# A four-layer network on one core: the scans of layer 0 written out as slots, with the other layers' work passed through them

## The chip, the core and the metric

The kernel runs on one core of a Trainium2 chip. A core has five engines that this text names as the profile does: PE (TensorE, matrix products, with its weight loads as PEld), DVE (VectorE), ACT (ScalarE), POOL (GpSimd) and SP (SyncE, which here only issues transfers). Each works through its own list of instructions in the order of the program and waits on semaphores for the others. The metric is the device time of one execution in microseconds; several executions are timed and their median is given.

## What is computed

The input x is 4 images of 384 channels and 48 x 48 pixels in float32. Four layers follow, each `x = x + layer(group_norm(x))`:

```python
# layer 0: a state-space scan over the 2304 pixels of an image
xz = xs @ in_proj_w.T;  xin, z = split(xz)          # 768 inner channels each
xin = silu(causal_conv4(xin) + conv_b)
dt, B, C = split(xin @ x_proj_w.T)                   # B, C: 16 states
dt = softplus(dt @ dt_proj_w.T + dt_proj_b)
h[t] = exp(dt[t] * A) * h[t-1] + dt[t] * B[t] * xin[t]   # per channel and state
y[t] = sum over states of h[t] * C[t]
out  = layer_norm(((y + xin * D) * silu(z)) @ out_proj_w.T)
# layer 1: 1x1 product, a filter on 8x8 patches in the frequency domain,
#          3x3 depthwise convolution, gelu(x1) * x2, 1x1 product
# layer 2: 11x11 depthwise convolution with kernels made of 4 points
# layer 3: 4 experts, relu(x @ w1 + b1) @ w2 + b2, top 2 by a gate per pixel, weighted
```

Layer 3 as the reference has it weighs expert e by whether *any* pixel has it first (or second), so that with all experts in use the weights of the two choices add to one for each expert and the layer is the plain sum of the four experts; the kernels compute the sum, look at a flag, and take the weighted way only if the flag asks for it.

## The kernel before

*The scans.* `scans` (line 411) runs over 20 pieces `i = (b, t)`: 4 images, each cut into five fifths of 460 or 464 pixels. The 768 inner channels are six groups of 128, taken as three pairs `p`; 16 states. So there are 20 x 96 = 1920 units `unit(i, m, s)` (line 618), each one scan of 128 channels over one fifth for one state. A unit is: ACT makes the decay `da = exp(dt * a)` in PSUM (line 629); POOL makes the drive `bu = u * B` (633); DVE scans (637), into `da` in place, or, for one unit in three, into `g`; the product with C is DVE's (643) for the two and POOL's (655) for the one, whose four transposes are added to `y` two units late (`late`); ACT copies the last column to `carry` (645, 654); PE adds `g` to `y` in PSUM by four transposes against the identity (`turned`, 587, recorded at line 591). `bc` holds B and C of a state, broadcast to all partitions by a transfer (625).

*The work around them.* Each fifth also has projections of the next (`project`, `project_z`), `gates` (silu), `expand` and `steps` (dt, u), `gate`, `out_proj`, `layer_norm` and `residual` of the one before. `plan(q, piece)` puts each piece behind unit q of the fifth, whole, from its first matmul to its last DVE operation. `scans` is a generator: it yields after each unit, and the main loop at line 1218 puts in pieces of the other layers, by weights and a steady rate, from unit 24 of an image on: `later(b-1)` (line 799, layers 1 and 2 and the gate's scores of layer 3 of the image before) and, ahead of it in the same list, `experts(b-2)` (line 1107, layer 3 of the image before that; the weights of all four experts are held, and `output` adds the four experts of a block of 144 pixels in one PSUM bank).

*The order on an engine* is not that of the text: a scheduling layer orders instructions by its own estimates and priorities, with `after` (line 395) and `high_priority` to bind a few, and `table_back` to return ACT to the table set of exp and ln.

*After the last scan* (line 1241 on) come `later(3)` mixed with `experts(2)`, then the routing, then `experts(3)`.

*Buffers:* PSUM has eight banks: three `da`, two `y`, two for all products (`mm`), one for long sums (`A`). In SBUF `g` has six buffers, `bu` three, `bc` four.

## Time and profile before

| | us |
|---|---|
| median of 3 runs | 5739.81 (5737.92 to 5743.05) |
| profiled execution, its own time | 5734.58 |
| its span, first to last instruction | 5732.5 |
| PE busy, PEld busy | 4867.7, 3805.7 |
| DVE busy | 4006.7 |
| ACT busy, POOL busy | 3044.1, 3104.5 |
| mean granted clock of PE | 0.884 of full |

A page of the profile gives each engine's busy time, then the span in 40 slices with a digit for the busy tenths of each engine, the clock that PE was granted and what the transfers did, then the chain of waits that ended last, and the groups of instructions: line, engine, operation, out<-in, how often, busy time, mean length in ns, and the idle time before them with what ended it. Matmuls are pipelined and their ends are modelled, so that a busy PE is not a PE at its peak. The records of a float32 matmul come in two for each instruction of the program; transposes come singly.

```profile
L1156 PE MATMUL ph<-xe,w 128*128 128x144 f32 x4608 | 620.8, 288 | 7.3 <-DVE dt L582 4.1
L1174 PE MATMUL pout<-hr,w 128*128 128x144 f32 x4608 | 617.8, 287 | 2.0 <-DVE xe L1185 1.9
...
L1164 ACT ACTIVATE hr<-ph,nb 128x144 f32<-128x144 f32 x768 | 235.4, 376 | 498.4 <-PE ph L1156 498.2
L895 DVE SCALAR_TENSOR_TENSOR dw<-pad,w_dw,dw 128x384 f32<-128x384 f32 x576 | 345.0, 614 | 20.2 <-ACT pad L883 16.1
```

These are the experts' two products, their relu, and the taps of the depthwise convolution of layer 1.

### The profile page before, as it was taken

The numbers are of one execution on the slowest core, as the hardware profiler recorded it, in microseconds if no ns is written. First come the engines' busy times: TensorE is split into PE (matmuls) and PEld (weight loads), VectorE is DVE, ScalarE is ACT, GpSimd is POOL, SyncE is SP. The second block draws the span as 40 slices with busy tenths as digits, with TensorE's granted clock in tenths as the row PEclk, the third lists the DMA queues.
The fourth block names the chain that finished last, engine by engine and source line by source line (L and its number), as shares of the span: only waits on it lengthen the run. The fifth ranks groups of instructions, "written<-read, shape, count | busy, mean of one in ns | idle before, by whom it ended". The sixth has DMA issues, their size and how long they took to land. (4 is left out here: it accounts for less than half of the span.)

```text
span 5732.5 us, 78378 instructions
## 1 busy us (share of the span) xinstructions
PE 4867.7 (85%) x27796; PEld 3805.7 (66%) x27796; DVE 4006.7 (70%) x5653; ACT 3044.1 (53%) x6658; POOL 3104.5 (54%) x2795
## 2 busy tenths in 40 slices
PE   6677777877788979999667988999867888999999
PEld 3555555544466657888444876989644576789999
DVE  5989898898897887667786777657787776351110
ACT  3555555556476665455554675545544675335321
POOL 3988888765576775556552666646553576000000
PEclk9778877978799989999768898999977799999999
DMA  4444444333344453333332335333332233311100
GB/s 134 137 143 144 141 127 142 124 114 116 98 150 138 128 178 124 109 109 121 101 112 84 114 117 173 107 95 116 113 100 70 95 128 126 113 56 39 47 23 26
DMA packets 396048, 634.78 MB, mean 111 GB/s; under 512 B 32374, under 2 KB 386790, under 8 KB 392191
## 3 DMA queue, kind: packets, MB, share of 16 engines
q1 hardware_dynamic: 382148, 618.58, 33.8%
q10 hardware_dynamic: 13498, 11.11, 0.6%
q8 instruction: 220, 3.60, 0.3%
q14 instruction: 182, 1.48, 0.1%
HBM read 571.80 MB, written 57.80 MB: 110 GB/s over the span
## 5 line engine op out<-in xcount | busy, mean ns | idle before, releaser
L633 POOL TENSOR_TENSOR bu<-u,bc 128x460 f32<-128x460 f32 (+1 forms) x1920 | 2209.2, 1168 | 1065.7 <-DVE g L637 488.3
L591 PE MATMUL y<-ident,g 128*115 128x128 f32 (+1 forms) x7680 | 1262.0, 313 | 433.1 <-DVE g L643 426.8
L591 PEld LDWEIGHTS y<-ident,g 128*115 128x115 f32 (+1 forms) x7680 | 1088.0, 199 | 673.3 <-DVE g L643 537.6
L629 ACT ACTIVATE da<-dt,a_neg 128x460 f32<-128x460 f32 (+1 forms) x1920 | 1221.9, 646 | 229.2 <-DVE g L643 141.7
L637 DVE TENSOR_TENSOR_SCAN da<-da,carry,bu 128x460 f32<-128x460 f32 (+1 forms) x1008 | 1158.0, 1172 | 152.1 <-ACT da L629 79.0
L655 POOL TENSOR_TENSOR g<-g,bc 128x460 f32<-128x460 f32 (+1 forms) x660 | 767.8, 1163 | 306.3 <-DVE g L637 122.9
L643 DVE TENSOR_TENSOR g<-da,bc 128x460 f32<-128x460 f32 (+1 forms) x1260 | 766.3, 628 | 90.2 <-PE y L591 76.8
L637 DVE TENSOR_TENSOR_SCAN g<-da,carry,bu 128x460 f32<-128x460 f32 (+1 forms) x528 | 617.5, 1169 | 129.6 <-PE y L591 92.6
L1156 PE MATMUL ph<-xe,w 128*128 128x144 f32 x4608 | 620.8, 288 | 7.3 <-DVE dt L582 4.1
L1174 PE MATMUL pout<-hr,w 128*128 128x144 f32 x4608 | 617.8, 287 | 2.0 <-DVE xe L1185 1.9
L1156 PEld LDWEIGHTS ph<-xe,w 128*128 128x128 f32 x4608 | 590.2, 192 | 24.1 <-issue 7.8
L1174 PEld LDWEIGHTS pout<-hr,w 128*128 128x128 f32 x4608 | 585.4, 190 | 17.7 <-issue 9.3
L1015 PE MATMUL pc<-band,row 128*128 128x162 f32 (+14 forms) x3456 | 494.5, 297 | 34.4 <-ACT row L1004 30.1
L1015 PEld LDWEIGHTS pc<-band,row 128*128 128x128 f32 x3456 | 472.0, 205 | 60.4 <-ACT row L1004 39.2
L645 ACT COPY carry<-da 128x1 f32<-128x1 f32 x1008 | 154.5, 157 | 671.9 <-DVE g L643 668.4
L1164 ACT ACTIVATE hr<-ph,nb 128x144 f32<-128x144 f32 x768 | 235.4, 376 | 498.4 <-PE ph L1156 498.2
L895 DVE SCALAR_TENSOR_TENSOR dw<-pad,w_dw,dw 128x384 f32<-128x384 f32 x576 | 345.0, 614 | 20.2 <-ACT pad L883 16.1
L515 PE MATMUL pinz<-xch,w_inz 128*128 128x460 f32 (+1 forms) x720 | 319.4, 581 | 38.6 <-DVE dt L582 14.3
L687 PE MATMUL po<-w_out,zs 128*115 128x384 f32 (+1 forms) x960 | 338.5, 502 | 12.8 <-DVE xc L504 7.2
L487 PE MATMUL pin<-xch,w_inx 128*128 128x463 f32 (+2 forms) x720 | 329.8, 595 | 11.5 <-DVE xc L504 6.0
L637 DVE TENSOR_TENSOR_SCAN da<-da,nil,bu 128x460 f32<-128x460 f32 x252 | 289.0, 1172 | 48.6 <-ACT carry L645 15.9
L1185 DVE SCALAR_TENSOR_TENSOR xe<-pout,b_sum,xe 128x144 f32<-128x144 f32 x192 | 58.9, 360 | 343.9 <-PE pout L1174 343.9
(173 smaller groups left out, 5331.9 us busy)
## 6 DMA issues: line engine op xcount, KB each, us to landing
bc<-bcd SPq DMA_DIRECT2D x768, 460.0 KB, 3.7
bc<-bcd SPq DMA_DIRECT2D x192, 464.0 KB, 3.6
xs<-x1d SPq DMA_DIRECT2D x24, 576.0 KB, 3.9
x2d<-xs SPq DMA_DIRECT2D x24, 576.0 KB, 2.9
x<-x2d SPq DMA_DIRECT2D x12, 1152.0 KB, 8.3
x3d<-x SPq DMA_DIRECT2D x12, 1152.0 KB, 6.1
xg<-x3d SPq DMA_DIRECT2D x24, 576.0 KB, 4.0
xe<-x3d SPq DMA_DIRECT2D x64, 216.0 KB, 2.6
```

The lines of the kernel that those rows point to most:

```text
L487: nc.tensor.matmul(ps[:, lo : halo + n], lhsT=w_inx[:, k, bass.ts(j, P)], rhs=c["x"][:, k, lo : halo + n], start=k == 0, stop=k == CT - 1,)
L591: nc.tensor.matmul(y[:w, bass.ts(k, P)], lhsT=src[:, bass.ts(k, w)], rhs=ident, is_transpose=True, start=start and k == 0, stop=stop, skip ...
L629: nc.scalar.activation(da[:, :n], c["dt", p][:, m % 2, :n], AF.Exp, scale=a_neg[:, m, s : s + 1])
L633: nc.gpsimd.tensor_mul(bu[:, :n], c["u", p][:, m % 2, :n], bc[:, 0, :n])
L637: nc.vector.tensor_tensor_scan(here[:, :n], da[:, :n], bu[:, :n], last if t else nil[:, 0:1], ALU.mult, ALU.add,)
L643: nc.vector.tensor_mul(g[:, :n], here[:, :n], bc[:, 1, :n])
L655: nc.gpsimd.tensor_mul(g[:, :n], here[:, :n], bc[:, 1, :n])
L687: nc.tensor.matmul(ps[:w, :C], lhsT=c["zs"][:, m, bass.ts(k, w)], rhs=w_out0[:, m, :], start=m == 0, stop=m == MT - 1,)
L895: nc.vector.scalar_tensor_tensor(v, src, w_dw[:, ct, k : k + 1], v, ALU.mult, ALU.add)
L1015: nc.tensor.matmul(d["acc2"][:, : BANDS[k] * W].rearrange("p (h w) -> p h w", w=W)[:, lo - edges[k] : hi - edges[k], xlo:xhi], lhsT=d["row ...
L1156: nc.tensor.matmul(ps[:, bass.ts(m, EB)], lhsT=d["w1"][:, e, k, bass.ts(m, P)], rhs=d["x", s][:, k, :], start=k == 0, stop=k == CT - 1,)
L1174: nc.tensor.matmul(d["o"][:, bass.ts(m, EB)], lhsT=d["w2"][:, e, k, bass.ts(m, P)], rhs=d["h", s, e][:, k, :], start=e == 0 and m == 0 and ...
```

## The change

Every piece of work is rewritten as a generator of *steps*. A step names its engine, and for PE a weight (about its us), a PSUM buffer that must be free, and a condition. `Ring` counts buffers as read or not; `Task` is one piece with the pieces that it needs; a `Lane` holds a queue of tasks and lets up to `width` of them move one step a slot, PE steps with weight against a credit that grows by `rate` a slot. The 1920 units become slots `u` in one loop under `manual_schedule`: the order of the text is the order on each engine.

In slot u: ACT steps of all lanes; copies of finished `y`; the scan of u with its product; the decay of u+2; the drive of u+3; POOL's product of u-1; the adds of u-4 (POOL's product) or u-2; then the PE, DVE, POOL and transfer steps of all lanes; `bc` seven units ahead. PSUM is now two `da`, two `y`, three `mm`, one `acc`; `g` has five buffers, `bc` five, `xch` two, and several buffers of layers 1 and 2 one instead of two.

Three lanes: `aux` for layer 0's own work (`plan` gives each task a first slot and what it needs), `one` for `later(b-1)`, `two` for `experts(b-1)`, which begins when `later(b-1)` has ended. In `experts` one expert runs over the whole image before the next: its weights alone are held, expert 0 writes x plus its part and all biases to `y3d` in HBM, each further one reads and adds to it, the last writes the output. The last image's layer 3 (`all_experts`) is as before. In layer 1 the taps of the third channel group come before those of the second, so that both gelus stand together, with one table change; the residual input is fetched again as `xr`. Weights for `fold` are issued on SP instead of ACT.

```diff
+class Lane:
...
+    def step(self, act, slot=0):
+        if not act:
+            self.credit = min(self.credit + self.rate, 4.0)
+        for task in self.active:
+            if task.ended:
+                continue
+            kind, weight, ring, when = task.next
+            if (kind == "act") != act or (weight and self.credit <= 0):
+                continue
+            if (ring and not ring[0].free(ring[1])) or (when and not when()):
+                continue
+            self.credit -= weight
+            task.move()
...
             def project(i, j):
...
+                yield ("pe", 0, (ring, 1))
...
-                ps = bank(f"pin{b}_{t}_{j}")
+                ps, r = ring.take(f"pin{b}_{t}_{j}")
...
+                yield ("act",)
...
+                yield ("dve",)
                 for k in range(halo):
...
+                ring.done(r)
...
+            def where(u):
+                i, q = divmod(u, LEN)
+                p, q = divmod(q, PAIR)
+                return i, p, 2 * p + q % 2, q // 2, q % 3 == 0
...
+            def scan(u):
...
+                here = g if slow else da
                 nc.vector.tensor_tensor_scan(
                     here[:, :n], da[:, :n], bu[:, :n], last if t else nil[:, 0:1],
                     ALU.mult, ALU.add,
                 )
...
+                if not slow:
+                    nc.vector.tensor_mul(g[:, :n], da[:, :n], live["bc", u // 2][:, 1, :n])
+                if t < NC - 1:
+                    nc.scalar.copy(last, here[:, n - 1 : n])
...
+                for u in range(N + 5):
...
+                    for lane in (aux, *lanes):
+                        lane.step(True, u)
+                    for h, e in ((1, u - 3), (0, u - 4)):
+                        if 0 < e < N and e % PAIR == PAIR - 1:
+                            collect(e, h)
+                    if u < N:
+                        scan(u)
+                    if u + 2 < N:
+                        decay(u + 2)
+                    if u + 3 < N:
+                        ready(u + 3)
+                        drive(u + 3)
+                    if 0 < u <= N:
+                        product(u - 1)
+                    add(u - 4, True)
+                    add(u - 2, False)
+                    for lane in (aux, *lanes):
+                        lane.step(False, u)
+                    if u % 2 and u + 7 < 2 * (N // 2):
+                        spread((u + 7) // 2)
...
+                def taps(ct):
+                    yield ("dve", 0, (accr, 1))
...
+                    room = 3 if slow_slot() else 2
+                    for k in range(9):
+                        if not room:
+                            yield ("dve",)
+                            room = 3 if slow_slot() else 2
+                        room -= 1
...
+            def block(s, e):
...
+                yield ("pe", 2.2, (ring, 1), lambda: hrs.free())
+                ps, r = ring.take(f"ph{b}_{s}_{e}")
+                h, hk = hrs.take(f"hr{b}_{s}_{e}")
+                product(ps, d["w1"], x)
...
+                yield ("act",)
...
+                yield ("pe", 2.2, (ring, 1))
+                ps, r = ring.take(f"pout{b}_{s}_{e}")
+                product(ps, d["w2"], h)
+                hrs.done(hk)
+                yield ("dve",)
+                if e:
+                    x, yk = d["y", s, e]
+                    y = x.rearrange("p c t -> p (c t)")
+                    nc.vector.tensor_add(y, ps[:, : CT * EB], y)
...
+        rings = of_experts("xe", 2), of_experts("ye", 2), of_experts("hr", 1)
...
+        ring, accr = psum("mm", 3), psum("acc", 1)
+        one, two = Lane(6), Lane(3)
+        one.rate, two.rate = 0.75, 0.62
...
+            holder[0], ring.n, accr.n = mm, 6, 2
+
+            one.queue += later(NB - 1, ring, accr)
+            one.rate, two.rate = 4.0, 0.45
```

After the scans the manual order ends; `later(3)` and `experts(2)` go through the lanes again, and the scheduling layer orders the engines there as before.

## The prediction

> **What bounds the kernel now.** I read the page first, then busy time by stage, then the costliest groups, then single instructions of VectorE in order of time.
>
> ```profile
> PE 4867.7 (85%) x27796; PEld 3805.7 (66%) x27796; DVE 4006.7 (70%) x5653; ACT 3044.1 (53%) x6658; POOL 3104.5 (54%) x2795
> ...
> PE   6677777877788979999667988999867888999999
> ...
> DVE  5989898898897887667786777657787776351110
> ...
> PEclk9778877978799989999768898999977799999999
> ...
> PE 11%; issue 4%; DVE 1%; DMA 0%; ACT 0%; SPq 0%; POOL 0%; DVEq 0%; ACTq 0%; POOLq 0%
> ```
>
> The reader sees two limits that take turns: where the PE row shows 9 the DVE row falls to 6 or 5, and where DVE shows 8 or 9, PE shows 6 to 8 at a lowered clock. The chain of waits is no help: it reaches back only to about 4789 us. So I cut the run at the first scan of each image (the starts of scans 0, 480, 960 and 1440 in the trace are 95.9, 1007.6, 2127.7 and 3487.2 us; the last scan ends at 4828.3) and asked for the busy time in these stretches.
>
> ```profile
> 95.00:1008.00 913.00, 680.55 (x2923) 476.39 (x2922) 826.67 (x1030) 525.59 (x1124) 768.27 (x686) 0.79 0.43 138
> 1008.00:2128.00 1120.00, 918.66 (x4559) 649.03 (x4557) 968.40 (x1346) 688.54 (x1457) 775.75 (x695) 0.87 0.40 129
> 2128.00:3487.00 1359.00, 1175.90 (x6904) 930.83 (x6902) 1000.32 (x1392) 756.44 (x1658) 778.53 (x698) 0.89 0.36 114
> 3487.00:4828.00 1341.00, 1160.08 (x6830) 912.25 (x6829) 978.01 (x1346) 742.75 (x1636) 773.37 (x693) 0.89 0.35 112
> 4828.00:5733.00 905.00, 879.38 (x6427) 804.39 (x6425) 202.63 (x472) 305.89 (x751) 4.82 (x15) 0.97 0.16 51
> ```
>
> The second and third fifth of image 2, by the same view:
>
> ```profile
> 2369.00:2640.00 271.00, 268.14 (x1921) 237.60 (x1920) 179.18 (x237) 141.52 (x355) 154.98 (x137) 1.00 0.35 109
> 2640.00:2945.00 305.00, 228.36 (x1035) 155.35 (x1034) 237.97 (x348) 156.12 (x328) 155.39 (x144) 0.81 0.34 108
> ```
>
> The columns are PE, PE's weight loads, DVE, ACT, POOL, clock, DMA share and rate. Image 0 is near VectorE's limit (91%). In images 1 to 3 VectorE is busy only 77% of 3820 us, although in total it has as much to do as any engine: experts(b-2) come in one burst (271 us with PE at 99%), then layers 1 and 2 come in another (305 us with DVE at 78%). The last stretch, 905 us, is PE at 97%.
>
> Of the groups, the drive's product on GpSimd and the readout's product on VectorE:
>
> ```profile
> L633 POOL TENSOR_TENSOR bu<-u,bc 128x460 f32<-128x460 f32 (+1 forms) x1920 | 2209.2, 1168 | 1065.7 <-DVE g L637 488.3
> ...
> L643 DVE TENSOR_TENSOR g<-da,bc 128x460 f32<-128x460 f32 (+1 forms) x1260 | 766.3, 628 | 90.2 <-PE y L591 76.8
> ```
>
> VectorE in order of time (start, length, both in us), inside image 0:
>
> ```profile
> 508.91 1.17 DVE L643 TENSOR_TENSOR g<-da,bc 128x460 f32<-128x460 f32 x2
> 509.98 1.17 DVE L637 TENSOR_TENSOR_SCAN g<-da,carry,bu 128x460 f32<-128x460 f32 x1
> 511.48 1.18 DVE L637 TENSOR_TENSOR_SCAN da<-da,carry,bu 128x460 f32<-128x460 f32 x1 [0.33 <-POOL bu L633]
> 512.75 0.64 DVE L643 TENSOR_TENSOR g<-da,bc 128x460 f32<-128x460 f32 x1
> ```
>
> And a line of the chain of waits that prices PE:
>
> ```profile
> 4986.08 2.21 PE pout L1174 x18
> ```
>
> A scan starts at 509.98, 0.10 us before the two products of 1.17 us from 508.91 end; but the product at 512.75 starts 0.09 us after the scan from 511.48 (1.18 us) ends, because it reads that scan's result. Over the whole trace, neighbours on DVE that don't need each other overlap by 85 to 93 ns (medians), a product right behind its own scan starts 91 ns after it (160 cases), and a tap or other fused multiply-add behind the one it continues starts 35 ns after it. PE at full clock: 18 matmuls of 144 columns in 2.21 us, 123 ns each. In the same way, start to start at full clock: a transpose of g 109 ns, 384 columns 323, 460 columns 387.
>
> **What the Trainium skill says.** "Perfetto Trace Analysis", Optimization Strategy: where the most contended engine changes over time, interleave the regimes; the stage lines above show two such regimes. "VectorE: DVE Perf Modes", The DRAIN you can't avoid: the next operation waits until the pipe is empty, and one that isn't held starts earlier; the trace agrees in both halves (91 ns behind, 90 ns ahead). "TensorE: Matmul & The Clock Gate", Part 1: the clock is half or full, and activity releases it; the trace shows 1.00 in the burst and 0.79 in image 0. "PSUM — Partial Sum Buffer", Engine vs sequencer instructions: the queues of ScalarE, VectorE and GpSimdE are strictly first in, first out; the DVE records start in the program's order throughout. So a step laid out too early holds up everything behind it on its engine.
>
> **The change part by part.**
>
> *Unchanged:* the 95.9 us before the first scan. Neither kernel has expert work of image 2 before the last scan in its PE order; after it stand later(3), experts(2), experts(3): 834 us of matmuls at full clock before, 828 after (same gaps, counts from the two orders). Before took 905 us for it. After adds in this tail 48 additions of `ye` (lines of 128x432, an estimate of 0.6 us from 128x384 and 128x460 rows, beside PE), one hidden buffer instead of three (about 0.1 us in 64 blocks, 7 us), and weights that are fetched per expert into the only buffer: the chain shows 10.3 us for such a fetch (`w<-in_L_w2T`). Mostly hidden behind later(3). I take 912 us, from 895 to 950.
>
> *DVE gets dearer.* Before, the scheduler put other work between most scans and their products (160 of 1260 stand directly behind). After, all 1260 do: 1100 x (91 + 93) ns = +202 us. More chained taps and similar pairs: about +55 us. Experts one by one: 96 additions of `ye` in the scan stage, less 90 ns overlap, 96 x 0.51 = +49 us, and small biases, +14. DVE's work from first to last scan, priced so: 3715 us before, 4036 after. By image: 816, 961, 980, 958 before; 875, 1037, 1075, 1049 after.
>
> *ACT and SP.* Table loads 141 to 91, 50 x 1.28 = 64 us less, off the path except that one gelu block per strip now stands in front of the decays. Silu still holds ACT for 2 x 2.5 + 2 x 1.28 = 7.6 us once a fifth. SP gets 470 more DMAs (`y3d`, `ye`, `xe` again, `xr`), about 100 MB on 635; the DMA engines are 34% busy, `bc` is fetched seven slots ahead (median landing 3.7 us against 2.3 us a slot): nothing.
>
> *PE work is spread.* By image at full clock, before and after: 494/502, 746/745, 1028/1039, 1011/1008. The totals don't move; their place inside an image does. Fifths of image 2: before PE 220, 265, 163, 201, 180 against DVE 169, 172, 235, 229, 175; after 191, 208, 196, 231, 213 against 208, 254, 230, 192, 191.
>
> *The sum.* Each engine's order is a list of slots: 1920 scans, with what stands between two of them. I priced every slot on each engine by the rows above, took groups of slots, and added the largest engine's total of each group: the group's size stands for how far engines can run apart (three to six buffers). With PE at 0.95 of full clock (0.87 to 0.89 in images 1 to 3, but 1.00 wherever PE is the limit), before gives 4599 us in groups of six and 4912 in groups of four; it took 4732. The mean of both, 4755, is within 0.5%. After gives 4485 and 4654, mean 4570: by image 911, 1127, 1286, 1247 against 912, 1120, 1359, 1341 measured before. The new layout has two `da` buffers for three, five `g` for six, and no scheduler to fill holes; I add 20 us and take 4590. Sum on the profile: 96 + 4590 + 912 = 5598 us against 5732.5. The profiled run was 5734.6 us (2 above its span), the median of the runs 5 more: 5605 us.
>
> **Rivals.**
>
> *In-order stalls (slower).* Place: ACT's lane steps stand in front of the decay for two slots on, and wait for PE steps of the slot before; every third product (line 839 of the new code) needs PE to be less than two slots behind. A slot with a project (6 x 0.387) and a block (18 x 0.123) is 5 us of PE with its transposes, double at half clock; ACT then stops, and DVE two slots later. Then engines run apart by two slots at most: groups of two give 5053 us, total 6061; half way to groups of four, 4850, total 5865. It decides from 0.07 us a slot on (4725 - 4590 over 1920). For it: DVE and PE are both loaded 2.1 us a slot in images 2 and 3. Against it: each step is laid one slot behind its producer, and `ring` lets three banks be in flight instead of two. I price it at 5880.
>
> *Balance pays in full (faster still).* PE stays at full clock since it is never idle long: groups of six at full clock, 4411, total 5426. Against it: image 0 has no work to spread and its DVE work grew by 59 us.
>
> *Gain eaten exactly.* DVE's +320 us equals what the spreading frees: 5728 to 5752 of the median, a narrow case. That the change doesn't do what it says I exclude: the orders show expert blocks of image 0 from slot 975 to 1427, beside later(1) from 1017 on.
>
> **How the numbers follow.** Likeliest, faster by 1 to 4%: 46%, 5605, own range 5480 to 5725. Faster still: 12%, 5430. Stalls: 37%, 5880, up to 6061. No change: 5%. Under 0.2% (12 us) this measurement can't tell from no change, as the three runs lie within 5 us. So faster 0.58, same 0.05, slower 0.37. The range leaves out some 15 in 100: it runs from 5420 (groups of six, full clock) to 6010 (most of the stalls' case).
>
> **What would show it.** Right: DVE busy over 84% in images 1 to 3 (77% now), no stretch with PE at 99% before the last scan, products directly behind scans with 91 ns between, image 0 between 900 and 940 us, the last stretch near 912. Wrong: ACT's decay or DVE's scan waiting for PE or ACT in each slot, clock under 0.85 in images 2 and 3, image 0 over 960 us, or a tail over 950 with PE waiting for weights.

## The result, and the profile after

The changed kernel takes 5829.09 us (median of 4, 5826.41 to 5839.95) against 5741.43 us (4 runs, 5737.92 to 5744.53) for the kernel before: ratio 1.0156, 95% interval 1.0139 to 1.0174. It is slower by 1.6%, where 5605 us, faster by 2.4%, was forecast. The profiled execution took 5827.99 us, its span is 5825.9.

The page of the changed kernel, the same rows as before:

```profile
PE 4837.9 (83%) x27796; PEld 3792.9 (65%) x27796; DVE 4239.6 (73%) x5806; ACT 3007.6 (52%) x6632; POOL 3119.5 (54%) x2795
...
PE   6677667777768898887889998888889998889999
...
DVE  5889888989988778788987778788977874631200
...
PEclk8788778788879898998989999888989999999999
...
PE 14%; DVE 1%; ACT 1%; DMA 1%; issue 0%; POOL 0%; SPq 0%; ACTq 0%; DVEq 0%; POOLq 0%
```

The swing between two limits inside images 1 to 3 is gone, as intended: DVE shows 7 to 9 from the second slice to the last scan, and PE 7 to 9 from the thirteenth slice on. The stretch after the last scan, called the tail below (the last seven digits), shows PE at 8 in three slices, where before it had 9 but for its start. DVE's total grew by 233 us. By stages, cut at the first scan of each image (87.7, 1061.3, 2248.8, 3570.5 us; last scan ends at 4852.3), with the columns of the prediction:

```profile
87.70:1061.30 973.60, 690.63 (x2960) 481.31 (x2960) 854.29 (x1036) 533.75 (x1122) 770.29 (x684) 0.79 0.41 129
1061.30:2248.80 1187.50, 923.80 (x4554) 657.57 (x4554) 1019.89 (x1348) 685.27 (x1450) 780.99 (x699) 0.85 0.39 126
2248.80:3570.50 1321.70, 1159.58 (x6948) 919.97 (x6948) 1064.45 (x1450) 746.00 (x1656) 782.23 (x698) 0.93 0.48 147
3570.50:4852.30 1281.80, 1127.22 (x6800) 897.15 (x6800) 1040.04 (x1395) 729.28 (x1631) 777.30 (x693) 0.92 0.47 145
4852.30:5826.00 973.70, 889.64 (x6384) 806.76 (x6384) 233.00 (x520) 290.23 (x741) 4.38 (x14) 0.96 0.28 82
```

| | before | forecast | after | after - before |
|---|---|---|---|---|
| before the first scan | 95.9 | 95.9 | 87.7 | -8 |
| image 0 | 911.7 | 911 | 973.6 | +62 |
| image 1 | 1120.1 | 1127 | 1187.5 | +67 |
| image 2 | 1359.5 | 1286 | 1321.7 | -38 |
| image 3 | 1341.1 | 1247 | 1281.8 | -59 |
| after the last scan | 904.2 | 912 | 973.6 | +69 |
| allowance for fewer buffers | | 20 | | |

So spreading the experts did pay in images 2 and 3, 97 us instead of the forecast 168, at a higher clock (0.93 and 0.92, from 0.89). Images without experts, 0 and 1, and the tail lost 198 us.

The records of VectorE give an account of the four images. Call its *own time* what it is busy, with the short gaps of up to 0.15 us between two of its instructions, and *waits* all longer gaps. From the first scan to the last its own time grew by 304 us (3798 to 4103; by image 53, 79, 88, 85), and its waits fell by 272 us (934 to 662; by image +9, -11, -126, -145). The difference is the 32 us that this stretch got longer. So the spreading freed VectorE of waits, and its dearer work is a little larger than what that freed. This is an account, and doesn't by itself show how much of the 304 us has to reach the time; the experiments ask that.

The product behind its scan, in order of time (start, length):

```profile
504.09 0.64 DVE L839 TENSOR_TENSOR g<-da,bc 128x460 f32<-128x460 f32 x1
504.64 1.17 DVE L834 TENSOR_TENSOR_SCAN g<-da,carry,bu 128x460 f32<-128x460 f32 x1
505.73 1.16 DVE L834 TENSOR_TENSOR_SCAN da<-da,carry,bu 128x460 f32<-128x460 f32 x1
506.98 0.64 DVE L839 TENSOR_TENSOR g<-da,bc 128x460 f32<-128x460 f32 x1
```

The scan at 505.73 ends at 506.89, its product starts 0.09 us later; the scans at 504.64 and 505.73 start 0.09 and 0.08 us before what precedes them ends. Over the trace all 1260 products start 91 ns (median) behind the operation before them; in the kernel before, where 523 had a scan of some unit directly ahead, the median of these began 86 ns before that scan's end.

What VectorE waits for over the whole run (who waits <- for whom: us, times, longest), the four that the experiments turn on:

```profile
DVE ye L1554 <- PE pout L1526: 291.2, 92, 21.4
...
DVE xc L654 <- ACT xc L648: 149.2, 93, 5.6
DVE da L834 <- ACT da L810: 103.4, 73, 6.3
DVE lst L901 <- ACT on L897: 79.3, 45, 5.6
```

The wait for `xc` was 45.8 us before. Both `xc` and `lst` are steps whose ACT half and DVE half stand in the same slot: the ACT steps of a slot come first, and the DVE step that needs one can follow at the end of the same slot. Before's waits of scans and products for PE to free `g` (115.8 and 76.8 us) are almost gone (2.4 and 0.4).

### The profile page after: what moved, and what is told of

It is laid out like the page before. It is cut to its first block, busy times and chain, and to the rows that moved or that the text cites. A ratio compares the mean times of both kernels' runs of the same rounds, so it can differ in the third digit from the quotient of the medians.

```text
span 5825.9 us, 79675 instructions
## 1 busy us (share of the span) xinstructions
PE 4837.9 (83%) x27796; PEld 3792.9 (65%) x27796; DVE 4239.6 (73%) x5806; ACT 3007.6 (52%) x6632; POOL 3119.5 (54%) x2795
## 5 line engine op out<-in xcount | busy, mean ns | idle before, releaser
L821 POOL TENSOR_TENSOR bu<-u,bc 128x460 f32<-128x460 f32 (+1 forms) x1920 | 2225.2, 1168 | 1567.1 <-DVE da L834 986.3
L810 ACT ACTIVATE da<-dt,a_neg 128x460 f32<-128x460 f32 (+1 forms) x1920 | 1243.9, 648 | 328.4 <-DVE g L839 231.0
L834 DVE TENSOR_TENSOR_SCAN da<-da,carry,bu 128x460 f32<-128x460 f32 (+1 forms) x1008 | 1181.0, 1172 | 145.0 <-ACT da L810 95.7
L839 DVE TENSOR_TENSOR g<-da,bc 128x460 f32<-128x460 f32 (+1 forms) x1260 | 803.2, 637 | 93.7 <-PE y L763 0.4
L834 DVE TENSOR_TENSOR_SCAN g<-da,carry,bu 128x460 f32<-128x460 f32 (+1 forms) x528 | 616.0, 1167 | 20.3 <-ACT da L810 17.3
L1526 PE MATMUL pout<-hr,w 128*128 128x144 f32 x3456 | 504.4, 302 | 33.4 <-ACT hr L1542 19.4
L1526 PEld LDWEIGHTS pout<-hr,w 128*128 128x128 f32 x3456 | 475.3, 203 | 61.2 <-ACT hr L1542 28.0
L1526 PE MATMUL ph<-xe,w 128*128 128x144 f32 x3456 | 495.0, 300 | 20.5 <-DMA xe<-x3d 7.4
L1526 PEld LDWEIGHTS ph<-xe,w 128*128 128x128 f32 x3456 | 469.6, 201 | 43.5 <-issue 16.5
L635 PE MATMUL pin<-xch,w_inx 128*128 128x463 f32 (+2 forms) x720 | 368.6, 656 | 34.8 <-DVE xc L654 22.9
L654 DVE SCALAR_TENSOR_TENSOR xc<-pin,conv_w,xc 128x460 f32<-128x460 f32 (+1 forms) x360 | 250.6, 696 | 157.8 <-ACT xc L648 149.2
L1542 ACT ACTIVATE hr<-ph,nb 128x144 f32<-128x144 f32 x576 | 176.1, 376 | 344.1 <-PE ph L1526 344.1
```

What stands on the lines that cost most here:

```text
L635: nc.tensor.matmul(ps[:, lo : halo + n], lhsT=w_inx[:, k, bass.ts(j, P)], rhs=c["x"][:, k, lo : halo + n], start=k == 0, stop=k == CT - 1,)
L810: nc.scalar.activation(da[:, :n], c["dt", p][:, m % 2, :n], AF.Exp, scale=a_neg[:, m, s : s + 1])
L821: nc.gpsimd.tensor_mul(bu[:, :n], c["u", p][:, m % 2, :n], live["bc", u // 2][:, 0, :n])
L834: nc.vector.tensor_tensor_scan(here[:, :n], da[:, :n], bu[:, :n], last if t else nil[:, 0:1], ALU.mult, ALU.add,)
L839: nc.vector.tensor_mul(g[:, :n], da[:, :n], live["bc", u // 2][:, 1, :n])
L1526: nc.tensor.matmul(ps[:, bass.ts(m, EB)], lhsT=w[:, k, bass.ts(m, P)], rhs=of[:, k, :], start=k == 0, stop=k == CT - 1,)
```

## Experiments

The theories: **A**, VectorE's dearer work (the product behind its own scan above all) decides. **B**, VectorE stands in line behind steps whose ScalarE or PE half is late. **C**, the tail's loss comes from weights in one buffer and a single `hr`; later **C2**, from PE standing in line there. **D**, engines can run apart by two to three slots only, so that each engine's work reaches the time by its share of the chain of waits. For D, I followed the chain back from the last scan of each image in the trace of the changed kernel: VectorE has some 471 of 973 us of it in image 0, 514 of 1187, 363 of 1322, 343 of 1282; PE has 647 and 633 us in images 2 and 3. (It is pieced together in many places where releasers are missing, so its shares are rough.)

Each ratio is to the kernel before, timed beside the run (medians of 5741 to 5749 us); differences below are of these ratios, times 5741, and good to some 14 us. The stages, in us, come from one trace each. e3 and e11 change nothing before the last scan, and there their single images differ by up to 7 us from the changed kernel: a smaller difference of one stage says nothing.

| | ratio | against after, us | image 0 | 1 | 2 | 3 | tail |
|---|---|---|---|---|---|---|---|
| after | 1.0156 | 0 | 973.6 | 1187.5 | 1321.7 | 1281.8 | 973.6 |
| e1 product later, SBUF | 1.0110 | -26 | 995.5 | 1177.6 | 1318.8 | 1269.7 | 973.1 |
| e2 step later | 1.0096 | -34 | 938.0 | 1167.8 | 1331.0 | 1298.6 | 971.2 |
| e3 tail weights | 1.0135 | -12 | 973.8 | 1187.5 | 1323.9 | 1287.0 | 959.2 |
| e4 add later | 1.0188 | +18 | 980.4 | 1194.5 | 1336.7 | 1282.8 | 967.3 |
| e5 third da, lead 3 | 1.0424 | +154 | 994.7 | 1217.6 | 1377.4 | 1339.1 | 976.8 |
| e6 product later, PSUM | 1.0201 | +26 | 952.9 | 1171.6 | 1355.0 | 1310.1 | 969.9 |
| e7 product behind steps | 1.0402 | +141 | 984.2 | 1229.6 | 1402.2 | 1341.9 | 930.4 |
| e8 smooth PE | 1.0141 | -9 | 974.0 | 1172.0 | 1320.7 | 1273.4 | 998.4 |
| e9 products in pairs | 1.0872 | +411 | 1059.8 | 1312.8 | 1433.4 | 1379.8 | 968.8 |
| e10 third da, lead 2 | 1.0374 | +125 | 985.3 | 1202.3 | 1368.6 | 1343.2 | 968.3 |
| e11 tail ahead | 1.0072 | -48 | 974.0 | 1190.1 | 1329.0 | 1275.2 | 928.5 |
| e12 carry first | 1.0603 | +257 | 1018.3 | 1264.8 | 1406.4 | 1344.3 | 970.4 |
| e13 as e6, carry behind | 1.0243 | +50 | 963.2 | 1175.5 | 1371.9 | 1306.5 | 975.3 |
| e14 dose | 1.0185 | +17 | 980.7 | 1194.9 | 1333.6 | 1283.8 | 976.4 |
| c2 = e2 + e3 + e11 | 1.0025 | -75 | 937.9 | 1170.6 | 1331.6 | 1298.6 | 931.1 |
| c3 = c2, half products | 0.9929 | -130 | 937.9 | 1167.8 | 1306.7 | 1266.2 | 929.8 |
| c4 = c3, all images | 0.9861 | -169 | 943.3 | 1135.8 | 1313.8 | 1268.0 | 929.8 |

**Moving the product, first try (e1), and its second half alone (e4).**

```diff
-                here = g if slow else da
+                here = g
-                if not slow:
-                    nc.vector.tensor_mul(g[:, :n], da[:, :n], live["bc", u // 2][:, 1, :n])
...
+            def readout(u):                    # called with u - 1, behind scan(u)
+                    nc.vector.tensor_mul(g[:, :n], g[:, :n], live["bc", u // 2][:, 1, :n])
...
-                    add(u - 2, False)
+                    add(u - 3, False)          # e4: this line and the copies of y alone
```

> The readout's product on VectorE is issued one slot later, behind the next unit's scan instead of its own; all scans write g, and the fast additions on PE follow one slot later too. Theory A (the 182 ns that each of 1260 products behind its own scan costs VectorE decide): 160 to 230 us less, 5600 to 5670, image 0 from 974 to between 905 and 925 us. Theory B (VectorE stands in line behind steps whose ScalarE or PE half is late): VectorE's records get denser, but only image 0, where VectorE is busy 88%, gets shorter; 30 to 70 us less in all, and the waits for xc, ye and lst (114, 84, 61 us in images 1 to 3) stay. The last stretch stays at 974.

> Only PE's fast additions are issued one slot later, the products stay behind their own scans: what the second half of the product's move does alone. Theories A and B: PE's wait for VectorE's g (about 150 us in images 1 to 3) falls below 60 us, the time changes by less than 30 us, since PE has time left there. If PE's waits for g are what holds up ScalarE and VectorE (a form of B): 50 to 120 us less.

e1 gave 26 us; image 0 got longer. The reason is in its groups, here of VectorE's product and GpSimd's drive between 1000 and 4850 us (count | busy, mean ns), first in the changed kernel, then in e1:

```profile
L839 DVE TENSOR_TENSOR g<-da,bc 128x460 f32<-128x460 f32 (+1 forms) x967 | 616.5, 638 | 69.0 <-DVE da L834 0.4
```

```profile
L821 POOL TENSOR_TENSOR bu<-u,bc 128x460 f32<-128x460 f32 (+1 forms) x1472 | 1708.7, 1167 | 1396.1 <-DVE da L834 873.9 <-DVE g L834 473.5 <-DMA bc<-bcd 26.0
```

```profile
L845 DVE TENSOR_TENSOR g<-g,bc 128x460 f32<-128x460 f32 (+1 forms) x973 | 782.0, 804 | 33.5 <-ACT carry L839 32.3
```

```profile
L821 POOL TENSOR_TENSOR bu<-u,bc 128x460 f32<-128x460 f32 (+1 forms) x1479 | 1971.3, 1339 | 1056.0 <-DVE g L834 932.4 <-DVE lnm L919 22.7 <-DMA bc<-bcd 22.2
```

With both sources in SBUF the product takes 804 ns instead of 638 (879 in image 0), and GpSimd's drive 1339 instead of 1167. 166 of the 182 ns saved are thus spent again, and e1 can't judge A. e4 cost 18 us, within the 30 that A and B allowed it, but not for nothing: in images 1 to 3 PE's wait for VectorE's `g` fell from 149.6 to 1.5 us, and its wait for GpSimd's `g` grew from 41.8 to 166.1. Later additions also keep `g` longer (a new wait of products for PE, 24.9 us in images 1 to 3).

**VectorE's step a slot later (e2).**

```diff
+            if kind == "dve" and clock[0] < task.moved + 1:    # slot of the task's last step
+                continue
```

> Every VectorE step of the other work is issued at the earliest one slot after the step before it in its task, instead of in the same slot as the ScalarE step that it needs. Theory B (standing in line): VectorE's waits for xc, lst, ye, uf, xe and zs (about 320 us in images 1 to 3) fall below 100 us, and the time falls by 120 to 250 us, to between 5580 and 5710. Theory A (VectorE's own dearer work): the waits move to other places, at most 30 us less; image 0 stays at 965 to 980.

34 us less, from images 0 and 1 (-36 and -20); images 2 and 3 got 9 and 17 longer. The waits that B names did fall, `xc` in images 1 to 3 from 114.2 to 10.1 us, `lst` from 61.5 to 10.1; but over the run:

```profile
DVE ye L1567 <- PE pout L1539: 383.9, 107, 18.6
...
DVE da L844 <- ACT da L820: 185.8, 89, 8.4
```

Against 291.2 and 103.4 above: most of the waits moved to the next place in line. In image 0 they went for good: VectorE's waits there fell from 90 to 55 us, which is the whole gain. B holds for a part of images 0 and 1, and its size was overrated three- to sevenfold.

**The tail (e3, e11).** e3 gives experts of image 2 a second buffer of weights, fetched ahead, and three `hr`. e11 is without these; it fetches x2 ahead and delays two products:

```diff
-            x2s = slots("x2", [P, HW], 1)
+            x2s = slots("x2", [P, HW], 2 if b == NB - 1 else 1)
...
+                    if b == NB - 1 and i == len(pairs) // 2 and ct + 1 < CT:
+                        put(("load2", ct + 1), lambda ct=ct + 1: load2(ct), "begin2")
...
+                if b == NB - 2:
+                    yield ("pool",)            # a round between relu and the output's product
...
+                if b == NB - 1:
+                    yield from wait(2)         # between the gated act and the strip's product
```

> Only the stretch after the last scan changes: experts of image 2 fetch the next expert's weights during the fifth block of the one before into a second buffer, and have three hr buffers instead of one. Theory C (weights in one buffer and a single hr cost the tail its 62 us over the forecast): last stretch 910 to 920 instead of 974, PE idle in it from 84 to under 30 us, time 5765 to 5778. Rival (the added y3d transfers and ye additions cost it): 10 to 25 us less, 5804 to 5819. The part up to the last scan stays at 4852 within 10 us.

> Only after the last scan: the x2 of the next channel tile is fetched half a tile ahead into a second buffer, and the output's product waits one round behind its relu, and the strip's product two rounds behind its gate. Theory C2 (in the last stretch PE stands in line: 23 us for rep after x2, 19 for hr, 15 for act, by its waits): these fall below 20 us together, last stretch 974 to between 920 and 940, 35 to 55 us less. Rival (the tail lost 69 us because experts' blocks are spread badly over later(3)): the waits go, the tail stays above 955.

PE's waits in the tail up to 5550 us, in the changed kernel, in e3 and in e11:

```profile
PE pr L1331 <- ACT rep L1320: 22.9, 5, 10.1
PE pout L1526 <- ACT hr L1542: 19.4, 35, 1.9
PE pb L1250 <- DVE act L1244: 15.4, 5, 5.7
```

```profile
PE pr L1331 <- ACT rep L1320: 20.9, 4, 9.6
PE pout L1526 <- ACT hr L1542: 18.0, 32, 1.9
```

```profile
PE pout L1531 <- ACT hr L1547: 18.6, 33, 1.9
...
PE pb L1252 <- DVE act L1244: 5.0, 2, 3.2
...
PE pr L1333 <- ACT rep L1322: 1.4, 2, 1.1
```

e3 gave 14 us of tail, C fails. In e11 the tail is 928.5, 45 us shorter, as C2 said; the waits for `rep` and `act` went (38.3 to 6.4), the one for `hr` stayed, so the round between relu and product did nothing. PE stood, five times and twice for about 10 us, at a transpose that needs the next channel tile's x2, with experts' products queued behind it. The account fits: in the tail PE is idle for 25 us in the kernel before, 84 in the changed one and 50 in e11, and busy for 879, 890 and 879. The tails of e7 and e8 in the table differ for another reason: PE work moved across the last scan (PE is busy there for 860 and 917 us).

**Banks (e5, e10).** A third `da` and two banks for other work, as the kernel before has it; e5 also issues the decay three slots ahead.

```diff
-                da = live["da", u] = mm.tile(..., tag="da")
+                da = live["da", u] = mm.tile(..., tag="da", bufs=3)
...
-        ring, accr = psum("mm", 3), psum("acc", 1)
+        ring, accr = psum("mm", 2), psum("acc", 1)
```

> A third PSUM bank for da and a decay issued three slots ahead instead of two; the bank comes from the other work, which has two instead of three. Theory D (what each engine may run ahead or behind is two to three slots, and the second da bank is one of the ties): VectorE's waits for da (97 + 33 + 17 + 13 us in images 1 to 3) fall below 80 us, and the time by 60 to 120 us, to between 5710 and 5770, all four images shorter. Theory A (VectorE's own dearer work): less than 20 us, the waits turn up at xc and ye. If three banks for the other work matter more: slower by 30 to 100 us, with PE waiting for VectorE's and ScalarE's reads of those banks.

> Control for the pair with three da banks: third da bank, two banks for other work, decay issued two slots ahead as in the changed kernel, product behind its own scan. If the product's place made the 132 us between those two runs: 5970 to 6000, as with a lead of three. If the decay's lead made it: 5850 to 5890.

Slower by 154 and 125. PE's waits in e5 show two that the changed kernel barely has:

```profile
PE pinz L667 <- DVE dt L743: 74.2, 20, 6.0
...
PE pin L635 <- DVE dt L743: 55.9, 18, 5.3
```

PE stands at a projection for a bank that VectorE's `dt` step must first give back. In the changed kernel the two waits together are 15 us. The split of the eight banks that the change made is worth over 100 us in this layout; the longer lead gains nothing.

**The order of two readers (e12), and what it means for the product.** ScalarE's copy to `carry` and VectorE's product both read the `da` bank.

```diff
+                if t < NC - 1:
+                    nc.scalar.copy(last, here[:, n - 1 : n])
                 if not slow:
                     nc.vector.tensor_mul(g[:, :n], da[:, :n], live["bc", u // 2][:, 1, :n])
-                if t < NC - 1:
-                    nc.scalar.copy(last, here[:, n - 1 : n])
```

> Only the copy of the scan's last column to carry on ScalarE is issued before VectorE's product instead of behind it. ScalarE's wait for that copy is shown as ended by the product (727 us in images 1 to 3); if the copy then waits for the scan alone, it comes 0.7 us earlier, but the decay behind it still waits for the product that frees its bank: within 15 us of the changed kernel. If the copy's wait is what makes decays late: 30 to 80 us less.

257 us more, for two lines exchanged. From the waits between 100 and 4900 us, first in the changed kernel, then here, and in order of time:

```profile
ACT carry L841 <- DVE g L839: 1003.0, 674, 6.5
```

```profile
DVE g L841 <- ACT carry L839: 758.6, 1003, 15.4
```

```profile
501.74 0.16 ACT L839 COPY carry<-da 128x1 f32<-128x1 f32 x1 [0.88 <-DVE da L834]
...
501.93 0.64 DVE L841 TENSOR_TENSOR g<-da,bc 128x460 f32<-128x460 f32 x1 [0.23 <-ACT carry L839]
...
502.61 0.65 ACT L810 ACTIVATE da<-dt,a_neg 128x460 f32<-128x460 f32 x1 [0.70 <-DVE g L841]
```

In this program the later of two readers of a bank waits for the earlier. The Trainium skill, "PSUM — Partial Sum Buffer", PSUM bank collisions raise a hardware error, says why it must: two engines may not access the same bank (in the same quarter of the partitions) at once, reads against reads included, and the hardware doesn't arbitrate. No run here lets them collide; the traces agree in that none of the 1008 products whose scan has a copy overlaps that copy, in either order (31 ns or more lie between them). With the copy first, each product waits at least 0.22 us for it, and much longer when ScalarE is behind; with the product first (the changed kernel), ScalarE waits, and its decay would wait for the product anyway. My expectation took that wait for idle time of ScalarE alone; it is a tie that works whichever way it is laid.

**Moving the product without the dearer form (e6, e13), in place (e7), in pairs (e9).**

```diff
+            def readout(u):                    # e6, e13: u - 1, behind scan(u); da bufs=3, mm 2
+                    nc.vector.tensor_mul(g[:, :n], da[:, :n], live["bc", u // 2][:, 1, :n])
+                    if G[i][1] < NC - 1:       # e13; in e6 the copy stays behind the scan
+                        nc.scalar.copy(carry[:, m, s : s + 1], da[:, n - 1 : n])
```

> As the first try at it, the fast product goes one slot later, behind the next unit's scan, but here the scan stays in place in PSUM, so that the product reads PSUM and SBUF as before; it takes the third da bank from the other work. The fast additions follow one slot later. VectorE should lose about 182 ns for each of 1260 products, 229 us in all, and GpSimd's product stay at 1167 ns. Theory A: 150 to 230 us less than the changed kernel (5600 to 5680). Theory D (VectorE has 27 to 48% of the chain of waits in each image): 229 us x 0.27 to 0.48 = 60 to 110 us less (5720 to 5770), most of it in images 0 and 1.

> Third da bank, two banks for other work, product one slot later from PSUM, and now the copy to carry behind the product, as in the changed kernel, so that the two readers of a da bank keep their order. Against the control with the product behind its own scan (5960) only the product's place differs. Theory A (VectorE's 182 ns for each of 1260 products, 229 us): 150 to 230 us less than the control, 5730 to 5810, images 0 and 1 shorter by 50 to 60 each. Theory D (the chain's share of VectorE, 27 to 48%): 60 to 110 us less, 5850 to 5900. Against the changed kernel it may still lose what the bank taken from the other work costs (5960 - 5829 = 131 us).

The trace of e13:

```profile
503.91 0.62 DVE L854 TENSOR_TENSOR g<-da,bc 128x460 f32<-128x460 f32 x1
504.45 1.16 DVE L840 TENSOR_TENSOR_SCAN g<-da,carry,bu 128x460 f32<-128x460 f32 x1
505.53 0.61 DVE L854 TENSOR_TENSOR g<-da,bc 128x460 f32<-128x460 f32 x1
```

Each product now starts 87 ns (median) before the scan ahead of it ends. Against the control e10, e6 is 99 and e13 75 us shorter: a third to two fifths of 229. D's range, not A's. By the traces VectorE's own time fell by 208 and 212 us, and 98 and 129 us of that came back as waits. The product's place isn't all that differs from e10, though: the additions of `g` come a slot later, as in e4, where that alone cost 18 us. PE's wait for GpSimd's `g` shows it, 112 us in e10 and 263 and 271 in e6 and e13. So the product's place alone may be worth more than the 75 to 99 us. e6 has the tie of e12 in it (products wait 126.9 us for copies in images 1 to 3, 8.6 in e13); why e13 is the slower one all the same isn't shown.

e7 puts the steps of other work between scan and product; e9 runs two scans, then both products:

```diff
+                for lane in (aux, *lanes):     # e7: VectorE's steps of the slot come here
+                    lane.step("dve", u)
                 if not slow:
                     nc.vector.tensor_mul(g[:, :n], da[:, :n], live["bc", u // 2][:, 1, :n])
...
+                    for v in (u - 1, u):       # e9, in place of the product, at the second scan
+                        if ("h", v) in live and (q % 3 == 2 or q == PAIR - 1):
+                            nc.vector.tensor_mul(live["g", v][:, :n], live.pop(("h", v))[:, :n], ...)
```

> VectorE's steps of the other work go between a unit's scan and its product instead of behind both; 590 of 1260 products then no longer stand directly behind their own scan, no buffer is added. 590 x 182 ns = 107 us less for VectorE. Theory A: 80 to 110 us less (5720 to 5750). Theory D: 107 x 0.27 to 0.48 = 30 to 50 us less, and some of it lost again, since the product now stands behind the step's wait for ScalarE: between 40 us less and 30 us more.

> Of each three units, one product is GpSimd's and two are VectorE's; here VectorE runs both scans first and then both products, so that 1200 of 1260 products no longer stand directly behind their own scan, with the two da banks and three banks for other work of the changed kernel. VectorE loses about 1200 x 182 ns = 218 us. From the third-bank pair of runs (5990 with the product behind its scan, 5857 one slot later) 58% of that should reach the time: 90 to 140 us less, 5690 to 5740, most in images 0 and 1. Rival: the first product now frees its da bank only after the second scan, so that the next decay is late by about 0.2 us in each of 640 triples: no gain, or up to 60 us more, with VectorE's wait for da doubled.

Both far slower. In e7 the product, and with it the next decay, queues behind a step that waits for ScalarE (ScalarE's waits for products: 1629 us, from 1238). In e9 the copy to `carry` stood ahead of the products, so e12's tie is in it (products wait 723 us for copies); if that cost is e12's 257 us, the remaining 154 are no gain either. They miss all expectations and say only that these two ways to delay the product fail with two `da` banks.

**Uneven slots (e8).** A lane waits while more than 1.0 us of earlier PE work is left at 2.5 us a slot; the lanes' rates go up to 4.0 and 1.0, so that this limit acts in their place.

> The PE steps of the other work are spread by their size: a lane waits while more than 1.0 us of PE work of earlier slots is left at 2.5 us a slot; nothing else changes, and all but about 23 us of PE work stay before the last scan. Theory D (engines may run apart by two to three slots only, so uneven slots cost): images 1 and 2 shorter by 15 to 40 us each, image 0 the same, 40 to 90 us less in all. Theory A: image 1 and 2 within 10 us of before, time within 20 us.

Images 1 and 3 fell by 15 and 8 us, image 2 by 1, the tail grew by 25. PE is busy for 27 us more in that tail, so what the images gained was mainly work left for later: no sign of what D was to gain.

**How much of VectorE's work reaches the time (e14, c3, c4), and whether the finds add up (c2).**

```diff
+                    nc.vector.memset(spare, 0.0)             # e14, behind each product; 128x128
...
-                return i, p, 2 * p + q % 2, q // 2, q % 3 == 0
+                return i, p, 2 * p + q % 2, q // 2, q % (3 if i < 10 else 2) == 0   # c3; c4: q % 2
```

> The changed kernel with one idle piece of work more on VectorE behind each of its 1260 products: a memset of 128x128, which nothing waits for, about 0.15 to 0.2 us each by the length of small VectorE rows, some 190 to 250 us in all (about 50 to 63 per image). It measures how much of VectorE's time reaches the clock where products stand behind their scans. Theory A: images 0 and 1 longer by the full dose, 2 and 3 by half or more: 150 to 220 us more. Theory D (VectorE's share of the chain of waits: 48, 43, 27, 27%): 70 to 100 us more.

The dose was much smaller than its records (165 ns each):

```profile
500.87 0.64 DVE L840 TENSOR_TENSOR g<-da,bc 128x460 f32<-128x460 f32 x1
501.48 0.17 DVE L841 MEMSET spare<- 128x128 f32 x1
501.56 1.05 DVE L835 TENSOR_TENSOR_SCAN g<-da,carry,bu 128x460 f32<-128x460 f32 x1
```

Where a scan follows (680 cases), from the product's end to that scan's end is 1118 ns here (median) against 1091 without the memset. Where other work follows it costs more: over the four images VectorE's own time grew by 76 us, 60 ns for each memset, and the four images by 28 us, while its waits fell by 48. So somewhat over a third of the dose reached the time. D's shares give 27 us for this dose; in images 0 and 1, where A has the full 34 us, it was 14. The change of the whole time, 17 us by the ratios and 32 by the spans, is as small as its error, so that this leans to D and proves little.

> The changed kernel with the three small moves that gave something alone: VectorE's steps one slot behind the step before them (-24), the last stretch's loads and products ahead (-41), expert weights of the last stretch into a second buffer with three hr buffers (-4). If they add up: 5760. If the stretch after the last scan and the scans share nothing, image 0 stays at 938 and the last stretch falls to 915 to 930.

> As c2, and from image 2 on GpSimd takes every second product instead of every third (160 more products, 0.64 us + 0.18 us each: 131 us less on VectorE, 187 us more on GpSimd, which is busy 60% there). If VectorE's work in images 2 and 3 reaches the time by its share of the chain of waits (27%): 35 us less than c2; if fully: 130 less; if PE alone sets these images: within 10 us of c2. Below 5743 it beats the kernel before too.

> As c3, but GpSimd takes every second product in images 0 and 1 too (VectorE 66 us less per image, GpSimd 93 us more, to about 92% of image 0's 938 us). If VectorE's work limits image 0: 898 to 915 us; if its in-order partners do, or GpSimd takes over: 930 or longer. Image 1: 1168 to between 1115 and 1150 by the same reasons. In all 40 to 90 us less than c3 by theory A, 20 us less to 20 more if GpSimd takes over.

c2 takes back 75 of the 90 us by which the changed kernel was slower; e2 and e11 make 82, so their gains add up within the error, and e3 adds nothing to e11. c3 beats the kernel before: 5698.13 us, ratio 0.9929 (0.9912 to 0.9947). c4 is the fastest of the study: 5668.59 us, ratio 0.9861 (0.9844 to 0.9879), faster by 1.4%. Its stages:

```profile
89.90:1033.20 943.30, 696.12 (x2956) 478.70 (x2956) 815.12 (x961) 528.91 (x1122) 847.91 (x758) 0.78 0.42 134
1033.20:2168.90 1135.70, 911.48 (x4506) 650.50 (x4506) 973.43 (x1265) 674.79 (x1446) 859.97 (x772) 0.85 0.41 129
...
4750.70:5680.50 929.80, 888.47 (x6479) 806.27 (x6477) 235.53 (x527) 293.75 (x748) 4.38 (x14) 0.98 0.30 90
```

Moving 75 products an image took 44 to 49 us of own time from VectorE (not the 66 that I expected). It shortened images 2 and 3 by 25 and 32 us (c3 - c2), image 1 by 32 (c4 - c3), and image 0 not at all: there VectorE's waits doubled, from 55 to 104 us, and GpSimd is now busy 848 of 943 us. So 0.5 to 0.7 of this work reached the time, in images 2 and 3 twice D's 27%, except where GpSimd is near its own limit. Not all of it need be VectorE's work: a unit whose product is GpSimd's scans into `g`, and its `da` bank is free right behind the scan, which also loosens the tie of e12. No run keeps the two apart.

## Why the prediction was wrong, point by point

- **What bounds the kernel; the change in PE's and ACT's work.** Right: two regimes, and spreading the experts evened them out. Fifths 2 and 3 of image 2 take 286.4 and 266.1 us, from 271.2 and 304.5, and in no fifth before the last scan is PE busy for more than 95%.
- **"DVE gets dearer", 202 us for products behind their scans.** The term was right as work: 1260 products, 91 ns behind, and all of VectorE's added work came to 304 us where 321 were forecast. How much of it has to be paid differs by run: over a third of e14's dose, a third to two fifths for the product's place (e6 and e13 against e10, with additions that come later), 0.5 to 0.7 for products that go to GpSimd (c3, c4).
- **The sum of the scan stage, 4590 us: the step that failed.** Measured 4764.6, with 62, 60, 36 and 35 us more than the forecast in the four images, less the allowance of 20. The term that was wrong is the size of the groups, which says how much standing idle the spreading removes. By the prediction's own prices the stretch was to lose 463 us in which VectorE isn't at work (4732 - 3715 before, 4590 - 4036 after); by the traces its waits fell by 272. The mean of six and four, which fitted the kernel before (4732 lies at groups of 5.1 between my 4599 and 4912), was carried over to a layout in which engines are tied closer. On the same scale 4765 lies between four slots (4654) and two (5053), at 3.4. The runs show ties that a count of buffers didn't: VectorE's half of a step in the slot of ScalarE's half (e2, 34 us), the two readers of a `da` bank (e12, 257 us for their order alone), and a projection that stands for a bank (e5, e10). The last two are what other layouts would cost; how much of the changed kernel's missing fall each tie makes stays open. The allowance of 20 us for fewer buffers and no scheduler was the place where they should have been priced.
- **Images 0 and 1** show it barest: nothing was spread there, VectorE's work grew by 59 and 76 us by my own count (53 and 79 by the traces), and I still forecast no change for image 0 and 7 us for image 1. The waits there changed by +9 and -11 us, so the loss of 62 and 67 us is, by account, VectorE's own time. Two moves take parts of it back: steps a slot later 36 and 20 us (e2), and the product's place 22 to 32 and 27 to 31 (e13, e6 against e10, in a kernel with another split of banks). That the two sum to about the loss is no proof, the less as e2 removes waits that the kernel before had too.
- **The tail, 912 us from 895 to 950.** Measured 973.6: mis-sized. The reasons that I gave, weights in the only buffer and one `hr`, are worth 14 us (e3). The loss is PE standing in program order at transposes and products whose inputs are late (e11, 45 us): the same mechanism that I quoted for the other queues and didn't apply to PE itself. The last 17 us over the forecast stay open; PE still waits 19 us for `hr` in e11.
- **Rivals.** The in-order stalls (5880) came nearest to 5829, and its sign was right. The place was right in kind, engines tied closer than the sum has it, but the third `da` bank and the longer lead, which should have helped, did not. My argument against it, that each step is laid one slot behind its producer, is wrong for VectorE's steps behind ScalarE's, which share a slot; e2 shows that. The third rival, a gain eaten by VectorE's work, is what the account of the four images looks like: 304 us against 272.
- **Signs.** Image 0 over 960 and a tail over 950 came true, with PE waiting for `rep`, `hr` and `act` rather than for weights; a clock under 0.85 in images 2 and 3 and a wait in each slot did not. DVE's share in images 1 to 3 is 3124 of 3791 us, 82%, short of the 84% named as right.

Open: how much of the 304 us of VectorE's own time causes the loss. The product's place (75 to 99 us), same-slot steps (34) and the gain of spreading can't be added from runs with different banks, and a kernel with three `da` banks *and* three for other work needs nine.

## What to carry to other kernels

When a scheduler's order is replaced by one written by hand, put each half of a step a slot behind the half on the other engine, fetch what PE's next transposes need before they are issued, and see which of two readers of a PSUM bank comes first. A sum by groups of slots that fits one layout doesn't fit another: count what ties engines together, slot by slot, before the group's size is chosen. And before moving work in place, look for an engine with room: 300 of the 1920 products moved to GpSimd gave 94 us (c4 against c2), where the best reordering of them gave 26 against the changed kernel (e1).

## What the runs showed of the hardware

- A float32 product on VectorE with both sources in SBUF took 804 ns beside GpSimd's products, with one source in PSUM 638; GpSimd's went from 1167 to 1339 ns (e1). The Trainium skill, "GPSIMD Engine Reference", Specifications, says that GpSimd shares its SBUF interfaces with VectorE and contends there with VectorE instructions that have two SBUF inputs; the trace agrees, and gives it a size. In e1 the 641 drives that no product overlaps took 1165 ns, the 1279 others 1421; in the changed kernel, with one source in PSUM, the two kinds took 1168 and 1167.
- A 128x128 memset of 165 ns between a product and the next scan delayed the scan's end by 27 ns only, and over all 1260 places it cost VectorE 60 ns on average (e14): the length of a record isn't its cost.
- A product that reads the result of the scan ahead of it started 91 ns after that scan's end (changed kernel, 1260 cases); laid behind another scan it started 87 ns before that scan's end (e13).
